# Filling the planned idle stretches of the matmul engine with unread identity products

## The chip, the cores and the metric

The kernel runs on one core of one Trainium2 chip. Times are device microseconds (us) from the first to the last instruction of that core and what lies around them; a shorter time is better. The core has a matmul engine (TensorE, PE in the profile; its weight loads are listed as PEld), a vector engine (VectorE, DVE), an activation engine (ScalarE, ACT), a general engine (GpSimd, POOL) and a queue that issues the DMAs (SyncE, SP). Each engine runs its own instructions in order and waits for others by semaphores. The profile also records the share of its full clock that PE is granted.

## The reference

The input x is 32 sequences of 256 tokens with 128 features, all fp32. Four blocks are applied, each behind a layer norm and each added to x:

```
x = x + attn_a(layernorm(x))   # delta-rule recurrence over the tokens, 128x128 state, gates
x = x + ffn(layernorm(x))      # silu(x Wg^T) * (x Wu^T), times Wd^T; integer weights / 127; hidden size 384
x = x + attn_b(layernorm(x))   # Mamba-2: in-projection, causal convolution of 4 taps, chunked state space, gated norm
x = x + ffn(layernorm(x))      # the same weights again
```

The recurrence of the first block, per sequence and token t, with k normalised and alpha, beta, g from sigmoids:

```
S = S @ (alpha_t * (I - beta_t * k_t k_t^T)) + beta_t * v_t k_t^T
o_t = (q_t @ S) * g_t
```

## The kernel before

**Tiling.** Two sequences (512 tokens, four tiles of 128) form a unit, and there are 16 units. A unit goes through attention (names ending in _a), the first feed-forward block (_f), the state-space block (_s) and the second feed-forward block (_h). Within the attention the recurrence is computed in blocks: a triangular system is inverted, first in blocks of 16 on DVE (tiles step_a and u_a, fed by rows_a through DRAM), then doubled on PE by transposes (pt_a) and pairs of products (p_a), with ACT copies between them (t_a). Layer norms end with a transpose of the normalised tile xn into xT_ps. Products are fp32 and each is two weight loads and two matmul instructions in the trace; transposes are one of each, with the identity matrix `ident` as the second operand.

**Memories.** Every PE result goes to one of eight PSUM banks (kind "ps", 512 fp32 per partition). A bank is taken by a tile at its first write and is free for the next tile when the last reader of the former is done.

**The order of the work.** No engine's order is written by hand. All operations of all units are first added as a graph (`add`), with an estimated busy time and latency for each. `matmul` estimates two passes of max(2n, 2 cols)/2.4 + 4.5 ns, which is 222 ns for a 128 x 128 product; `transpose` takes 109 ns. `Planner.run` (line 333) then simulates the engines: it repeatedly places the operation that can start first, by a key with units staggered (`SHIFT`, `STAGE`), and a start time that is the latest of the engine being free, the operands being ready, and a bank being free; for the first operation of a bank, also all operands that anything put into this bank will need (`b.gate`, line 385). The result is a start time `op.start` for each operation. The list is sorted by it (line 441), and the instructions are emitted in that order; each engine's program order is therefore the plan's. Times in the plan are used for the order alone: on the chip an instruction starts when its engine is there and its semaphores are.

Line 238 issues every product, line 251 every transpose, line 275 every DVE operation, lines 259 and 261 the ACT copies and activations, line 292 POOL's and line 302 the DMAs. Since these are helpers, one must go by the names of the tiles.

Of the kernel before, what the change touches and what calls it, by code (L numbers as in the profile page):

```python
# [18 lines left out]
P = 128  # L19
# [128 lines left out]
class Planner:  # L148
# [13 lines left out]
    RATE = 270.0  # L162
    LANES = 8
    CUT = 150.0
    KEEP = 3900.0
    SIZES = {"ps": 512, "m": 512, "l": 1024, "t": 64, "s": 32, "d": 512, "g": 8192, "b": 384, "e": 12288}

# [35 lines left out]
    def add(self, eng, busy, late, emit, outs, ins, table=None, after=(), lock=False):  # L203
        op = Op()
        op.eng, op.busy, op.late, op.emit, op.table, op.lock = eng, busy, late, emit, table, lock
        op.unit, op.n, op.stage = self.unit, len(self.ops), self.stage
        op.preds, op.succs, op.bufs = {p.n: p for p in after}, [], []
        op.moves, op.cut, op.batch = 0.0, 0, ()
        for v, write in [(v, False) for v in ins] + [(v, True) for v in outs]:
            if not isinstance(v, View):  # L210
                continue
            bits = v.bits()
            for other, obits, lanes, owrite in v.buf.seen:
                if (
                    other is not op and (write or owrite) and bits & obits
                    and lanes[0] < v.lanes[1] and v.lanes[0] < lanes[1]
                ):
                    op.preds[other.n] = other
            kept = v.buf.kind == "c" and not v.buf.again
            assert self.setup or not (kept and write)  # L220
            if self.setup or not kept:
                v.buf.seen.append((op, bits, v.lanes, write))
            if v.buf.kind == "c" and v.buf.tile is None:
                v.buf.tile = self.pools["c"].tile(list(v.buf.dims), v.buf.dtype, tag=v.buf.name, name=v.buf.name)
            if v.buf.kind != "c" and v.buf not in op.bufs:
                op.bufs.append(v.buf)
        for p in op.preds.values():
            p.succs.append(op)
        self.ops.append(op)
        return op  # L230
# [53 lines left out]
    def pool(self, name, out, *args, ins=(), cost=None, **kw):  # L284
        n = _count(out)
        if cost is None:
            cost = {
                "tensor_tensor": 1.66 * n + 149, "tensor_scalar": n + 260, "tensor_copy": n + 190, "memset": 0.97 * n + 60,
            }.get(name, n / 2 + 100)

        def emit():
            getattr(self.tc.nc.gpsimd, name)(real(out), *map(real, args), **{k: real(v) for k, v in kw.items()})  # L292

        lock = name == "tensor_tensor" and n > NT
        self.add("POOL", cost, 40, emit, [out], list(args) + list(kw.values()) + list(ins), lock=lock)
# [16 lines left out]
    def gates(self):  # L312
# [7 lines left out]
        for b, ops in users.items():  # L320
# [4 lines left out]
                    of.add(self.ops[n])  # L325
            b.gate = {p for op in ops for p in op.preds.values()} - of

    def at(self, unit):

        late = max(0, unit - (self.units - 3))  # L330
        return (unit - late + late * self.LAST) * self.period + self.SHIFT[unit]

    def run(self):
# [18 lines left out]
        free = dict.fromkeys(engines, 0.0)  # L352
# [9 lines left out]
        order = []  # L362
        while len(order) < len(ops):
            best = None
            for e in engines:
# [31 lines left out]
                if e == "PE":  # L397
                    same = [((k[0] + (self.KEEP if op.cut != cut else 0), k[1]), t, op) for k, t, op in same]
                pick = min(same, key=lambda x: x[0])
# [3 lines left out]
            t, op = best  # L403
# [4 lines left out]
            if op.eng == "PE":  # L408
                t += self.CUT if op.cut != cut else 0.0
                cut = op.cut  # L410
# [28 lines left out]
                oldest += 1  # L439
        self.span = max(op.done for op in ops)  # L440
        order.sort(key=lambda op: (op.start, op.n))
        with self.tc.manual_schedule():
            for op in order:
                for b in op.bufs:
                    if b.tile is None:
                        size = self.SIZES[b.kind]
                        flat = self.pools[b.kind].tile([1 if b.kind in "dge" else P, size], BF16 if b.kind in self.HALF else F32, tag=f"{b.kind}{b.slot[1]}", name=b.name + self.mark)
                        b.tile = flat[:, : b.size]
                        if len(b.dims) > 2:
                            names = " ".join(f"d{i}" for i in range(1, len(b.dims)))  # L450
                            b.tile = b.tile.rearrange(
                                f"p ({names}) -> p {names}", **{f"d{i}": b.dims[i] for i in range(2, len(b.dims))}
                            )
                op.emit()


# [5 lines left out]
def hybrid_block(ctx: ExitStack, tc: tile.TileContext, ins: dict, out: bass.AP):  # L462
# [36 lines left out]
    pl = Planner(tc, pools, period=17900.0, window=6)  # L499
# [6 lines left out]
            pattern=pattern, channel_multiplier=by,  # L506
        )

    ident = pl.const([P, P], "ident")
    pool("memset", ident, 0.0)  # L510
    select(ident, ALU.not_equal, 0, [[-1, P]], 1, fill=1.0)

# [186 lines left out]
    def power_half(dst, src, mul, add):  # L699

        n = dst.shape[1]
        pool("tensor_scalar", dst, src, mul, add, ALU.mult, ALU.add, cost=277)
        pool("tensor_tensor", dst, dst, neg_half[:, :n], ALU.pow, cost=350 + 160 * n)
# [33 lines left out]
    def attention(g, x):  # L737
# [117 lines left out]
        for b in range(NBLK):  # L855
            at = slice(b * BLOCK, (b + 1) * BLOCK)
            pl.dma(
                blocks[0, :].rearrange("(b t j i) -> b j t i", b=NBLK, t=NT, i=BLOCK)[b, :, :, :],
                diag[:, :, at].part(at), late=1400,
            )  # L860
        rows_n = pl.buf("l", [P, NT, BLOCK, BLOCK], f"rows_{n}")
        spread = rows_n.rearrange("p t j i -> p (t j i)")
        for b in range(NBLK):
            at = slice(b * BLOCK, (b + 1) * BLOCK)
            size = NT * BLOCK * BLOCK
            pl.dma(
                spread.part(at),
                blocks[0, b * size : (b + 1) * size].via(lambda ap: ap.partition_broadcast(BLOCK)),
                late=2100,
            )  # L870
# [374 lines left out]
```

## Time and profile before

| | |
|---|---|
| median of 3 runs | 804.33 us (802.57 to 809.08) |
| the profiled execution | 806.73 us |
| its span, first to last instruction | 804.9 us |
| mean granted clock of PE | 0.975 |
| instructions | 16786 |
| busy: PE, PEld | 744.7 us, 616.5 us |
| busy: DVE, ACT, POOL | 684.3, 597.2, 364.0 us |

Busy times are of one profiled execution. PE's records overlap one another, since a matmul starts before the last one has ended, and their ends are modelled; so a stretch in which PE reads as busy can still have room. A wait is listed as the instruction that waited, the engine and tile whose end released it, the total, the number of times and the longest. The chain is followed back from the last instruction to what released each step. A window's row gives start and end, length, and then for each engine the busy time and the instructions, the granted clock, the share of the DMA engines and GB/s.

### The profile page before, as it was taken

To read this page: it belongs to the slowest core of one execution; us is meant where nothing else is said; L and a number is where in the kernel's file an instruction comes from. 1 tells how busy PE (TensorE), PEld (TensorE's weight loads), DVE (VectorE), ACT (ScalarE), POOL (GpSimd) and SP (SyncE) were. 2 spreads that over 40 slices of the span, in tenths; PEclk is the share of its full clock that TensorE was granted. 3 is DMA by queue.
4 is the path that set the end of the run, shared out by engine and by line. 5 is a ranking of instruction groups with operands and counts; after the bars stand their busy time and mean duration, and the time that the engine had idled before them with its cause. 6 is when DMAs were issued, how large, how long until landed. Compare 5 with 4: busy or idle time off the path is not lost.

```text
span 804.9 us, 16786 instructions
## 1 busy us (share of the span) xinstructions
PE 744.7 (93%) x5485; PEld 616.5 (77%) x5485; DVE 684.3 (85%) x2386; ACT 597.2 (74%) x1443; POOL 364.0 (45%) x597
## 2 busy tenths in 40 slices
PE   5958999899999999999999999899999999998886
PEld 4646886687878888877988878686789988776775
DVE  4794799989988889889999689989898778999964
ACT  5833467979687877779787798897955578997862
POOL 8994332262452815514732634646631123243550
PEclk9976999999999999999999999999999999999999
DMA  5221110010110002101011002011201000000001
GB/s 145 82 68 42 29 42 1 5 33 1 56 30 24 22 7 67 42 27 33 18 30 31 27 15 58 16 45 44 67 4 43 14 5 1 5 15 5 13 10 44
DMA packets 42159, 25.48 MB, mean 32 GB/s; under 512 B 18448, under 2 KB 37840, under 8 KB 42064
## 3 DMA queue, kind: packets, MB, share of 16 engines
q1 hardware_dynamic: 41056, 24.13, 11.1%
q8 instruction: 45, 0.74, 0.4%
q14 instruction: 50, 0.41, 0.2%
q10 hardware_dynamic: 1008, 0.20, 0.1%
HBM read 19.16 MB, written 5.14 MB: 30 GB/s over the span
## 4 chain that ended last, share of the span: by engine, by line
PE 52%; DVE 20%; ACT 15%; POOL 5%; issue 3%; DMA 2%; SPq 1%; ACTq 0%; DVEq 0%; POOLq 0%
PE p_a L238 6%; PE fy_f L238 5%; DVE cy_s L275 4%; PE fy_h L238 4%; PE fg_f L238 3%; ACT L261 3%; PE sy_ps_s L238 3%; PE so_s L238 2%; PE fu_f L238 2%; PE pc_s L238 2%; PE fg_h L238 2%; PE fu_h L238 2%; PE pt_a L251 2%; DVE u_a L275 2%; PE cb_ps_s L238 2%
## 5 line engine op out<-in xcount | busy, mean ns | idle before, releaser
L275 DVE SCALAR_TENSOR_TENSOR cy_s<-pc_s,cw,cy_s 128x510 f32<-128x510 f32 (+2 forms) x192 | 137.6, 731 | 2.9 <-ACT cy_s L261 2.3
L261 ACT ACT_TABLE_LOAD x66 | 84.7, 1283 | 9.9 <-DMA x<-in_L_attn_a_x_dram 5.8
L238 PE MATMUL fy_f<-wdT,hT_f 128*128 128x128 f32 x384 | 74.5, 280 | 0.0
L238 PE MATMUL fy_h<-wdT,hT_h 128*128 128x128 f32 x384 | 72.1, 281 | 0.6 <-DVE hT_h L275 0.3
L238 PEld LDWEIGHTS fy_f<-wdT,hT_f 128*128 128x128 f32 x384 | 61.4, 191 | 6.3 <-issue 3.6
L238 PE MATMUL pc_s<-xT_s,w_xbc 128*128 128x512 f32 x128 | 64.5, 599 | 1.3 <-ACT gT_s L259 0.7
L238 PEld LDWEIGHTS fy_h<-wdT,hT_h 128*128 128x128 f32 x384 | 59.1, 191 | 8.1 <-issue 4.3
L275 DVE TENSOR_TENSOR step_a<-rows_a,u_a 128x16 f32<-128x16 f32 (+14 forms) x240 | 51.7, 216 | 7.5 <-DMA rows_a<-blocks_a 3.1
L275 DVE TENSOR_TENSOR u_a<-u_a,step_a 128x16 f32<-128x16 f32 (+14 forms) x240 | 54.3, 227 | 3.9
L261 ACT ACTIVATE cy_s<-pc_s,cb,cw 128x512 f32<-128x512 f32 x64 | 48.3, 779 | 9.3 <-PE pc_s L238 9.1
L292 POOL TENSOR_TENSOR xd_s<-xt_s,dt_s 128x512 f32<-128x512 f32 x32 | 33.2, 1045 | 42.9 <-ACT xt_s L259 42.2
L238 PE MATMUL so_s<-w_out,gT_s 128*128 128x128 f32 x256 | 45.8, 290 | 1.9 <-DVE cy_s L275 1.2
L238 PEld LDWEIGHTS so_s<-w_out,gT_s 128*128 128x128 f32 x256 | 39.7, 204 | 6.6 <-ACT cy_s L261 1.4
L261 ACT ACTIVATE sc_s<-cy_s 128x512 f32<-128x512 f32 x64 | 38.9, 636 | 3.6 <-DVE cy_s L275 1.9
L275 DVE SCALAR_TENSOR_TENSOR sm_s<-pl_s,cb_s 128x512 f32<-128x512 f32 x64 | 41.3, 680 | 0.3 <-ACT pl_s L261 0.2
L292 POOL TENSOR_TENSOR sy_s<-sy_s,yo_s 128x256 f32<-128x256 f32 x32 | 24.6, 773 | 35.5 <-DVE sy_s L275 14.2
L238 PEld LDWEIGHTS p_a<-t_a,neg_a 128*128 128x128 f32 x256 | 36.4, 203 | 5.5 <-ACT t_a L259 3.7
L238 PE MATMUL p_a<-t_a,neg_a 128*128 128x64 f32 x256 | 38.1, 280 | 1.8 <-DVE x L275 1.3
L238 PEld LDWEIGHTS p_a<-x_a,t_a 128*128 128x128 f32 x256 | 36.6, 201 | 3.7 <-ACT t_a L259 2.3
L238 PE MATMUL p_a<-x_a,t_a 128*128 128x64 f32 x256 | 37.9, 274 | 1.0 <-ACT t_a L259 1.0
L259 ACT COPY t_a<-pt_a 128x256 f32<-128x256 f32 (+1 forms) x64 | 20.2, 316 | 24.0 <-PE pt_a L251 22.9
L275 DVE TENSOR_TENSOR hT_f<-fth_f,fu_f 128x512 f32<-128x512 f32 x48 | 31.2, 681 | 7.3 <-PE fu_f L238 4.8
(253 smaller groups left out, 2420.7 us busy)
## 6 DMA issues: line engine op xcount, KB each, us to landing
rows_a<-blocks_a SPq DMA_DIRECT2D x128, 64.0 KB
x<-in_L_attn_a_x_dram SPq DMA_DIRECT2D x16, 256.0 KB
dec_a<-row_a SPq DMA_DIRECT2D x16, 256.0 KB
out_dram<-x SPq DMA_DIRECT2D x16, 256.0 KB
blocks_a<-neg_a SPq DMA_DIRECT2D x128, 4.0 KB
cuts_s<-cut_s SPq DMA_DIRECT2D x48, 8.0 KB
sums_t<-cuts_s SPq DMA_DIRECT2D x32, 12.0 KB
sums_s<-cuts_s SPq DMA_DIRECT2D x16, 24.0 KB
```

Source lines behind the costliest of these rows:

```text
L238: self.tc.nc.tensor.matmul(real(out), lhsT=real(lhsT), rhs=real(rhs), start=start, stop=stop)
L251: self.tc.nc.tensor.transpose(real(out), real(in_), real(ident))
L259: self.tc.nc.scalar.copy(real(out), real(in_))
L261: self.tc.nc.scalar.activation(real(out), real(in_), func, bias=real(bias), scale=real(scale), **kw)
L275: getattr(self.tc.nc.vector, name)(real(out), *map(real, args), **{k: real(v) for k, v in kw.items()})
L292: getattr(self.tc.nc.gpsimd, name)(real(out), *map(real, args), **{k: real(v) for k, v in kw.items()})
```

## The change

After the order is fixed, a new step walks through PE's operations in it. It keeps the time at which PE is free in the plan (starting at 1700 ns). Where the next operation's planned start is more than `IDLE` = 300 ns later, where its bank has not been written before by another PE operation, and where it isn't one of the half-width products (`op.cut`), the operation is marked with a number of extra products: int(gap x 0.7 / 223). When the program is emitted, these are issued just ahead of the operation: the identity (as stationary and as moving operand, at most 128 columns) into the start of the same bank. Nobody reads them; the operation then writes over them. The order of all other instructions is that of before, and no tile, bank, copy or DMA is added or moved.

```
+    IDLE, WARM = 300.0, 0.7
...
+    def keep_busy(self, order):
+        written, free = set(), 1700.0
+        for op in order:
+            if op.eng != "PE":
+                continue
+            bank = next(b for b in op.bufs if b.kind == "ps")
+            gap = op.start - free
+            if gap > self.IDLE and bank not in written and not op.cut:
+                op.warm, op.bank = int(gap * self.WARM / 223), bank
+            written.add(bank)
+            free = op.start + op.busy
...
         order.sort(key=lambda op: (op.start, op.n))
+        self.keep_busy(order)
...
-                        b.tile = flat[:, : b.size]
+                        b.flat = b.tile = flat[:, : b.size]
...
+                for _ in range(op.warm):
+                    n = min(P, op.bank.size)
+                    one = self.ident.real()
+                    self.tc.nc.tensor.matmul(op.bank.flat[:, :n], lhsT=one, rhs=one[:, :n], start=True, stop=True)
                 op.emit()
...
-    ident = pl.const([P, P], "ident")
+    ident = pl.ident = pl.const([P, P], "ident")
```

More of the change, by code (lines that the diff above doesn't have):

```diff
@@ L207, in add @@
         op.preds, op.succs, op.bufs = {p.n: p for p in after}, [], []
-        op.moves, op.cut, op.batch = 0.0, 0, ()
+        op.moves, op.cut, op.batch, op.warm = 0.0, 0, (), 0
         for v, write in [(v, False) for v in ins] + [(v, True) for v in outs]:
```

## The prediction

> **What bounds the kernel now.** I read the page first: engine totals, slices, the chain that ended last.
>
> ```profile
> PE 744.7 (93%) x5485; PEld 616.5 (77%) x5485; DVE 684.3 (85%) x2386; ACT 597.2 (74%) x1443; POOL 364.0 (45%) x597
> PEclk9976999999999999999999999999999999999999
> PE 52%; DVE 20%; ACT 15%; POOL 5%; issue 3%; DMA 2%; SPq 1%; ACTq 0%; DVEq 0%; POOLq 0%
> ```
>
> The matmul engine (PE) carries half of the chain and VectorE (DVE) a fifth. The granted clock is full almost everywhere; only the third and fourth of the 40 slices (about 40 to 80 us) fall to 0.7 and 0.6. Next I cut the span where the clock changes (columns: window, length, busy time and instruction count of PE, PE weight loads, DVE, ACT, POOL; then the clock, DMA share, GB/s):
>
> ```profile
> 48.00:58.20 10.20, 6.28 (x21) 5.02 (x22) 9.90 (x28) 2.82 (x6) 10.08 (x16) 0.50 0.21 67
> 65.00:78.60 13.60, 12.30 (x54) 11.27 (x55) 4.12 (x16) 3.65 (x11) 8.53 (x11) 0.50 0.22 61
> 242.50:246.00 3.50, 3.30 (x10) 2.62 (x11) 3.50 (x10) 3.48 (x8) 0.00 (x0) 0.52 0.00 0
> 730.60:734.00 3.40, 3.24 (x10) 2.36 (x11) 3.19 (x12) 2.42 (x8) 1.85 (x3) 0.50 0.00 0
> 754.50:758.00 3.50, 3.50 (x28) 3.28 (x29) 2.81 (x5) 3.44 (x5) 0.00 (x0) 0.52 0.00 0
> 771.50:775.00 3.50, 3.50 (x19) 3.36 (x17) 2.20 (x5) 1.87 (x2) 2.61 (x4) 0.51 0.02 5
> ```
>
> So PE runs at half clock in two long stretches near the start and four short ones. Each was preceded by a thin window; PE's records alone, busy in the 3.4 us ahead of a drop:
>
> ```profile
> 239.10:242.50 3.40, 2.15 (x10) 0.99 0.00 0
> 727.20:730.60 3.40, 1.39 (x13) 0.99 0.00 0
> 751.10:754.50 3.40, 1.84 (x10) 0.99 0.00 0
> 768.10:771.50 3.40, 1.59 (x24) 1.00 0.00 0
> 61.60:65.00 3.40, 1.53 (x7) 0.99 0.04 4
> ```
>
> Records 41 to 63% busy went before every drop. Last, the waits of PE over the whole run (total, times, longest), and the chain where the clock is half:
>
> ```profile
> PE kT_ps_a L251 <- POOL k_a L292: 4.5, 1, 4.5
> PE xT_ps_a L251 <- ACT xn_a L261: 3.3, 1, 3.3
> PE xT_ps_h L251 <- ACT cb_s L259: 2.2, 1, 2.2
> PE xT_ps_f L251 <- DVE cy_s L275: 1.9, 2, 1.2
> PE fu_f L238 <- ACT fth_f L261: 1.3, 1, 1.3
> ```
> ```profile
> 64.96 1.98 PE p_a L238 x8
> 67.39 1.99 PE p_a L238 x8
> 69.95 1.11 PE pt_a L251 x4
> ```
>
> The first two wait for their own operands. The other three wait for something the matmul doesn't read (an xT transpose reads neither cb nor cy, fu_f doesn't read fth_f): the last reader of the PSUM bank that the new tile takes over. That difference decides what a filler is worth.
>
> **What the Trainium skill says.** (1) "TensorE: Matmul & The Clock Gate", section "What's actually happening": the array's clock is halved after an idle window of about 3.4 us, and restored after a busy one. The trace agrees: the short dips last 3.4 to 3.5 us, the long ones are 10.2 (three windows) and 13.6 (four). (2) Same page, "Part 4: PE-mode transpose": transposes don't count as PE activity in the same way. The trace fits without proving it: from 65.0 to 78.6 records are busy 12.30 of 13.6 us, transposes (pt_a, kT_ps_a) among them, and the clock stays at half for four windows. (3) "Perfetto Trace Analysis", section "Identifying the Most-Contended Engine": matmul busy time is a poor measure of headroom, weight-load busy time a better one; here they are 93% and 77%, so PE has free places that the first hides. (4) "PSUM — Partial Sum Buffer", section "Terms": two engines on one bank's quadrant at once is an error, so a filler has to wait for the bank's readers as the real product does. The bank waits above agree.
>
> **The change, part by part.** The order, the buffers, every other instruction and every DMA queue stay: keep_busy only reads the finished plan, and nothing is moved.
>
> *What is added.* Ahead of an operation that is the first to write its bank, where the plan leaves over 300 ns, int(0.7 x gap / 223 ns) products of the identity with itself. Each fp32 product is two weight loads and two matmuls.
>
> *Price of one.* Eight p_a matmuls (four products) follow one another at 84.86 to 85.80 in 0.94 us with the clock full, so 0.23 us; at half clock eight start at 71.58 and the next product at 73.34, so 0.44 us. I use 0.223 warm (the plan's figure, which this supports) and 0.44 cold.
>
> *How many.* The plan's gaps are in no view; I take PE's idle in the trace as the nearest, and put both ends. Between 80 and 720 us PE has 24 us of idle (615.97 busy of 640) in some 45 gaps; a record also holds about 0.16 us of latency (a p_a matmul lasts 0.27 to 0.28 us and starts 0.11 after the last) that the plan counts as gap: 24 + 45 x 0.16 = 31 us. All filled: 0.7 x 31 / 0.223 = 98 products. Rounding down, gaps ahead of an operation that isn't first in its bank, and a plan that is tighter than the run cut it; ends 30 and 120, I take 50. Up to 80 us: 5.8 us ahead of the first product (plan start counted from 1.7) make 18, the waits of 4.5 and 3.3 make 14 and 10, the small ones some 12. After 720 us: six waits, 7 us, up to 22.
>
> *Cost in the middle.* 50 x 0.223 = 11 us of PE work. A filler ahead of an operand wait lies in idle time, if plan and run agree; one ahead of a bank wait can start only when the bank is free, and then delays the real product by its whole length, with all later PE work queued behind it, and ACT or DVE waiting for its result. I take half as late, 5.5 us, and let PE's share of the chain (52%) pass it on: **+3**. Ends: 30 products, a third late: +1; 120, three quarters late, 70% passed on: +14.
>
> *Gain at 65 to 79.* This is on the chain: p_a at half clock, 54 matmul records in 13.6 us, of which half would be saved if PE were the only thing there; less the ACT and DVE pieces, about 6 us. Whether the clock holds at 65.0 depends on the window 61.6 to 65.0. Fillers ahead of pvq_a (0.9 us of wait), pd_a (0.4) and p_a (0.55), some six products, 1.3 us, would bring its 1.53 us of records to 2.9 of 3.4, above every window that dropped. I take **-4**: six by two chances in three. Ends 0 and -6. What is late next is the DVE step and update chain and the SP issues at 93, which follow from these products and so move with them.
>
> *Gain at 48 to 58:* nothing. The waits there become filled, but DVE is busy 9.90 of 10.2 us and carries the chain (step_a, u_a, e_a); if that cover were gone, the cold kk_a group (2.77 us against 1.47 a little later) would be worth 1.3 us.
>
> *Before the first product:* PE idles until 8.05 us and then works cold until 17.2. The 18 fillers take 18 x 0.44 = 8 us cold, less once warm: the first real product is 0.3 us late at most by my sum, but pv_a and pk_a on the chain (12.86 to 16.5) may run at full clock, worth 1.8 us. From 19.5 to 37 the chain is POOL without a break, and hides most of it: **-1**, ends -2 and +1.
>
> *The end, 720 to 802.* Fillers ahead of xT_ps_h and pl_s (bank waits, 2.2 and 1.2 us) come after the release: 7 + 4 products, 2.5 us, with half on the chain, 1.3 us. Against that, three dips at half clock cost up to 1.7 us each; so_s at 754.5 and 772.7 is on the chain. Fillers ahead of pf_s (operand wait, 1.8 us) can prevent the last one. Together **-1**, ends -4 and +3.
>
> *Sum:* +3 - 4 - 1 - 1 = -3 us. The profiled execution took 806.73 us (span 804.9 plus 1.8 around it), so 803.7; the median of the runs is 804.33, 2.4 below the profiled one. I give it on the median: **801**.
>
> **Rivals.**
> A (the forecast, 0.41): the clock gain at the start outweighs a modest PE load: 801.
> B, slower (0.29): bank waits. Most plan gaps are bank waits, or don't fall where the run idles, so the fillers queue in front of real work. 100 products, 22 us, three quarters late, 70% passed on: +12, less 3 of clock gains: 813. For it: of PE's five longest waits three are for a bank's reader, and PE is half of the chain. Against: 24 us of idle exist in the middle. It decides from about 60 late products on (60 x 0.223 x 0.52 = 7 us against 6 of gain).
> C, faster (0.24): all fills land in idle time and all six stretches run at full clock: -1.5 at the start, -6 at 65 to 79, -3.5 later, +1: 794. For it: each drop follows a thin window; against: bank waits at the last dips.
> D (0.06): the change does little: the plan has few gaps above 300 ns, or the clock drops all the same, as the transposes may not count: 804.
>
> **How the numbers follow.** About 1% is what a measurement of this kernel can tell from no change (the three runs span 802.6 to 809.1). The range takes in most of B and C: 792 to 815; it leaves out the worst end of the middle's cost (+14 with no gain, 818) and C with its last dips all gone. Faster by over 1% (below 796.3): most of C and the gain's upper end in A, 0.29. Slower by over 1% (above 812.4): half of B and a bit, 0.23. Within: 0.48.
>
> **What would show it.** The page's PE row: 5485 plus twice the products, 5700 to 5900. Clock: 1.00 in 65 to 79 and 48 to 58 if A or C is right; then the p_a groups take about 1.0 us and not 1.97, and everything after 80 us starts some 4 us sooner. For B: identity products that start right after a bank's release, with a real product directly behind, and a lead at 80 us that melts by 720. The forecast is wrong if the clock at 65 still drops, if that lead is swallowed by DVE or POOL (idle ahead of rows_a would grow), or if the plan holds over 100 products in the middle.

## The result: slower by 0.6%, and the profile after

Twenty-two runs of each kernel give a median of 809.28 us after (806.14 to 813.02) and 804.76 us before. The ratio is **1.0058**, with a 95% interval of 1.0040 to 1.0076: slower by 3.2 to 6.1 us. (Here and below a ratio is estimated from the single runs of both kernels; it can differ from the quotient of the two medians by about 0.1%.) The profiled execution of the changed kernel took 809.79 us (span 808.0), against 806.73 us (span 804.9) before: 3.1 us more. Its mean granted clock rose all the same, from 0.975 to 0.990.

The page after: busy time and instructions, PE's clock in 40 slices, and the shares of the chain that ended last.

```profile
PE 761.3 (94%) x5713; PEld 635.4 (79%) x5713; DVE 684.8 (85%) x2386; ACT 597.2 (74%) x1443; POOL 364.4 (45%) x597
PEclk9997999999999999999999999999999999999999
PE 48%; DVE 22%; ACT 16%; POOL 6%; issue 3%; DMA 3%; SPq 2%; DVEq 0%; ACTq 0%; POOLq 0%
```

PE has 228 instructions more, so 114 extra products. DVE, ACT and POOL do the same work as before. The third slice is now at full clock, the fourth still shows 0.7. The windows of the kernel after that still run at half clock, apart from the first 7.2 us (the clock's record starts there; that PE is slow ahead of it shows in the weight loads of the extra products, 333 ns instead of 192) and the last 2 us, in which PE does nothing (columns as in the prediction: window, length, busy time and instructions of PE, PE weight loads, DVE, ACT, POOL, then the clock):

```profile
61.80:72.10 10.30, 10.10 (x41) 8.24 (x41) 4.61 (x18) 4.06 (x16) 8.80 (x15) 0.50 0.31 74
734.30:737.70 3.40, 3.40 (x17) 3.34 (x17) 1.36 (x4) 0.00 (x0) 1.08 (x2) 0.50 0.00 0
```

The stretch at 48 to 58 is gone, the one that the prediction wanted gone (65 to 79 before) has moved to 61.8 and lasts three windows instead of four, and one of the four short dips is left in this execution. PE's waits after (total, times, longest):

```profile
PE pvq_a L239 <- DVE neg_a L276: 3.3, 1, 3.3
PE xT_ps_h L473 <- ACT cb_s L260: 2.2, 1, 2.2
PE xT_ps_f L473 <- DVE cy_s L276: 1.7, 2, 1.1
PE fu_f L473 <- ACT fth_f L262: 1.2, 1, 1.2
```

Line 473 is that of the extra products. **They wait for the same releases as the real operations did**: xT_ps_h still waits 2.2 us for cb_s, fu_f 1.2 us for fth_f, about as long as before (2.2 and 1.3). Such a wait isn't filled; the products merely come behind it. And a new long wait has appeared, pvq_a for neg_a. It was 0.9 us before, and has no extra product ahead of it.

**Where the time went.** I followed the start of the same instructions in both traces. The changed kernel is 1.1 us ahead at 40 to 50 us, 3.5 at 59, again 1.1 at 63, when the wait for neg_a is over, and 2.8 us ahead at 80 (the product wq_a starts at 78.49 instead of 81.27). The lead is 0.7 us at 140 to 160, 0.4 at 200 to 230 and 1.4 at 250 to 290; then it is behind by 1.2 at 340, 1.5 at 480, 2.7 at 520, 3.0 at 640 to 700, 5.9 at 740 and 3.0 again at 780. So 2.8 us are won by 80 us and 5.8 us lost from there to 700. Of these 5.8 us, 2.6 fall in 296 to 340 us, where no extra product stands; they come back under the hardware below. At extra products the lead shrinks, or the lag grows, by 1.6 us from 133 to 148 us (12 of them, ahead of pz_s, xT_ps_f, pt_a, fg_f and fu_f), by 0.3 at 188 (2 ahead of so_s), 0.6 at 520 to 523 (5 ahead of so_s and p_a) and 0.1 at 554 (1 ahead of cs_s): together 2.6 us. What else is lost, some 1.6 us in four small steps, has no extra product or a single one at its place, and 0.9 us is won where the dip of before at 242 us is missing.

In the plan, 58 products stand in the first 70 us and 56 later. Of the 56, **39 stand ahead of an operation whose planned start is within 50 ns of the time at which its PSUM bank comes free**, and 17 ahead of other operations. By the trace, 35 of the 56 run between 80 and 720 us, 23 of them of the bank kind.

### The profile page after: what moved, and what is told of

It reads as the page before. It is cut to its first block, busy times and chain, and to the rows that moved or that the text cites. A ratio compares the mean times of both kernels' runs of the same rounds, so it can differ in the third digit from the quotient of the medians.

```text
span 808.0 us, 17232 instructions
## 1 busy us (share of the span) xinstructions
PE 761.3 (94%) x5713; PEld 635.4 (79%) x5713; DVE 684.8 (85%) x2386; ACT 597.2 (74%) x1443; POOL 364.4 (45%) x597
## 4 chain that ended last, share of the span: by engine, by line
PE 48%; DVE 22%; ACT 16%; POOL 6%; issue 3%; DMA 3%; SPq 2%; DVEq 0%; ACTq 0%; POOLq 0%
PE p_a L239 6%; DVE cy_s L276 4%; PE fy_f L239 4%; PE fy_h L239 3%; PE pc_s L239 3%; ACT L262 3%; PE fg_f L239 2%; PE fu_h L239 2%; PE fu_f L239 2%; PE fg_h L239 2%; PE sy_ps_s L239 2%; PE so_s L239 2%; SPq L303 2%; DVE u_a L276 2%; PE pt_a L252 2%
## 5 line engine op out<-in xcount | busy, mean ns | idle before, releaser
L276 DVE TENSOR_TENSOR step_a<-rows_a,u_a 128x16 f32<-128x16 f32 (+14 forms) x240 | 53.4, 223 | 10.4 <-DMA rows_a<-blocks_a 5.3
L239 PE MATMUL so_s<-w_out,gT_s 128*128 128x128 f32 x256 | 42.9, 276 | 0.0
L239 PEld LDWEIGHTS so_s<-w_out,gT_s 128*128 128x128 f32 x256 | 37.3, 192 | 3.3 <-issue 1.2
L262 ACT ACTIVATE pl_s<-pl_s 128x512 f32<-128x512 f32 x64 | 33.8, 581 | 5.3 <-PE pl_s L239 5.2
```

The lines of the kernel that those rows point to most:

```text
L239: self.tc.nc.tensor.matmul(real(out), lhsT=real(lhsT), rhs=real(rhs), start=start, stop=stop)
L262: self.tc.nc.scalar.activation(real(out), real(in_), func, bias=real(bias), scale=real(scale), **kw)
L276: getattr(self.tc.nc.vector, name)(real(out), *map(real, args), **{k: real(v) for k, v in kw.items()})
```

## The experiments

Two theories. **T1 (bank):** a stretch in which PE is idle because no bank is free can't be filled through that same bank. The products start at the release, and the real product starts later by their whole length. **T2 (load):** any extra product costs some PE time, as plan and run don't agree on where the gaps are; a cheap wait and a dear one don't differ. Beside these, for the early part: **T3**, the gain was to be had, but the planned gaps didn't put products in front of the window that decided it.

The kernels below differ from the changed kernel only in which operations get products. For this, `run` records when the plan found the bank free. All compute the whole reference, and ratios are to the kernel before, on the same chip.

### The early products alone

```
+                    if b.kind == "ps":
+                        op.slot_at = b.slot[0]
...
+            for_bank = op.start - op.slot_at < 50.0
-            if gap > self.IDLE and bank not in written and not op.cut:
+            if gap > self.IDLE and bank not in written and not op.cut and op.start < 70000.0:
```

> Only the 58 products of the first 70 us of the plan stay. Theory (what costs is a product that waits for the bank of the product behind it, later on): PE is full-clocked from about 7 us, p_a is reached some 2.8 us sooner as in the changed kernel's profile, and nothing takes it away later: 2 to 3 us under the kernel before, ratio 0.9965. Rival (extra PE work costs wherever it stands, about half of 0.223 us each): 58 products, 13 us, hidden in the start or not, +2 us or more. Second rival (a start that is sooner is swallowed by DVE or POOL): within 0.1% of before.

Measured: 802.89 us, ratio 0.9980 (0.9952 to 1.0009), so -1.6 us, and no change isn't excluded. In this execution the clock was at half from 62.1 to 86.0 us, and wq_a started at 82.07, later than in the kernel before:

```profile
62.10:86.00 23.90, 23.51 (x101) 21.36 (x100) 9.08 (x36) 7.25 (x27) 9.72 (x15) 0.50 0.15 35
```

The early products don't hold the clock at 62 us. The lead of 2.8 us that the changed kernel showed at 80 us is the property of one execution.

### Only the products ahead of bank waits, and only the others

```
-            if gap > self.IDLE and bank not in written and not op.cut:
+            if gap > self.IDLE and bank not in written and not op.cut and for_bank:
```

> Only products ahead of an operation that the plan holds back for a free bank (start within 50 ns of the time at which the bank comes free): 39 products, all after 115 us of the plan. Theory: each starts when the bank is free and delays the real product by its whole 0.223 us: 8.7 us of delay, of which nearly all reaches the end, less some 3 us of clock dips near the end that they prevent: +5 to +6 us, ratio 1.006 to 1.0075. Rival (extra PE work costs about the same wherever it stands): 39 of 114 products, a third of the measured +4.6 us, so +1.5 us.

```
+            if gap > self.IDLE and bank not in written and not op.cut and not for_bank:
```

> The other 75 products: those of the first 70 us and 17 later ones whose operation the plan holds back for operands or for the bank's other operands. Theory: 2 to 4 us under the kernel before, ratio 0.995 to 0.9975, as fast as the early ones alone or a little faster. Rival (cost by number): 75 of 114, +3 us, ratio 1.004.

Measured: the 39 bank products alone give 810.53 us, **1.0083** (1.0059 to 1.0107), +6.7 us, a little over what was expected. The 75 others give 805.19 us, 1.0009 (0.9988 to 1.0030), +0.7 us. The loss is therefore in the 39, as T1 wants. The second run missed its expectation of 0.995 to 0.9975: the 17 late products that aren't ahead of bank waits eat the 1.6 us of the early ones, or the intervals hide it; this pair doesn't tell. The two kernels share out all 114 products of the change, and 6.7 + 0.7 = 7.4 us is 2.7 more than the 4.7 of the change. The intervals (1.9, 1.7 and 1.4 us to either side) just cover that gap, so a part can't be read more finely than to 2 or 3 us from medians.

### The bank products doubled

```
-                op.warm, op.bank = int(gap * self.WARM / 223), bank
+                op.warm, op.bank = int(gap * 2 * self.WARM / 223), bank
```

(with `for_bank` as above: 87 products)

> As the run with only the products ahead of bank waits, but with twice the share of the gap: 87 products in place of 39. Theory: the cost grows with PE time behind the release: 87 x 0.223 = 19.4 us, less the same 3 us of dips: +14 to +16 us, ratio 1.018 to 1.020. Rival (the cost is one of a wait moved onto another instruction, or of the program's length, not of PE time): about as the single share, +5 us.

Measured: 815.67 us, 1.0130 (1.0095 to 1.0165), +10.5 us. A miss: 48 further products are 48 x 0.223 = 10.7 us of PE time and cost only 3.8 us. One place explains a part of it. These are PE's instructions ahead of xT_ps_h in this run and in the changed kernel (start, duration, engine, line, tile, count, and the idle before with its releaser):

```profile
740.78 2.94 PE L477 MATMUL xT_ps_h<-ident 128*128 128x128 f32 x24 [2.18 <-ACT cb_s L260]
743.56 0.60 PE L252 MATMUL xT_ps_h<-ident,xn_h 128*128 128x128 f32 x4
```
```profile
734.09 2.81 PE L473 MATMUL xT_ps_h<-ident 128*128 128x128 f32 x12 [2.20 <-ACT cb_s L260]
736.70 1.06 PE L252 MATMUL xT_ps_h<-ident,xn_h 128*128 128x128 f32 x4
```

Twelve products (24 instructions) at full clock delay the transposes by 743.56 - 740.78 = 2.78 us, six at half clock by 736.70 - 734.09 = 2.61. By the medians the further products weigh less than the first ones: 39 pass on 6.7 of 8.7 us, 87 pass on 10.5 of 19.4 us. The traces don't bear this out at the places of the products. Up to 720 us the lag behind the kernel before grows there by 2.6 of 5.1 us with the 23 products of the undoubled rule, and by 7.5 of 11.8 us with the 53 of the doubled one. What the doubled kernel's trace lacks is loss at other places: nothing from 285 to 345 us, where that of the undoubled kernel loses 2.0 us without a product. Six runs and one trace don't settle whether the miss comes from that.

### The bank products of the middle alone, and as many ahead of operand waits

```
+            if gap > self.IDLE and bank not in written and not op.cut and for_bank and op.start < 660000.0:
```

> Of the 39 products ahead of bank waits, only the 23 of the middle (plan 115 to 660 us); the 16 of the last part are left out. Theory: 23 x 0.223 = 5.1 us of delay behind a release, about two thirds of it passed on: +3 to +4 us, ratio 1.004 to 1.005. Rival (the cost of the 39 is that of the last part, where six products ahead of xT_ps_h run at half clock): +1 us or less, ratio under 1.0015.

The counterpart has no planned products. A list of tile names gives 23 of them, all between 80 and 720 us, to operations that wait for their own operands in the trace:

```
+    HOLD = {"p1_a0_64": 1, "py_a0": 1, "p3_a2_64": 1, "py_a2": 3, "pt_a5_16": 4, "py_a4": 1, "xT_ps_f4": 4, ...}
...
+            if bank not in written and bank.name in self.HOLD:
+                op.warm, op.bank = self.HOLD[bank.name], bank
```

> 23 products in the middle, as many as in the run with the bank waits of the middle alone (ratio 1.0063), but ahead of other operations: 13 of which PE waits in the trace of before for an operand that they read, with their bank free (p1_a0_64 1, py_a0 1, p3_a2_64 1, py_a2 3, pt_a5_16 4, py_a4 1, xT_ps_f4 4, p3_a5_64 1, pz_s7_0 1, z_a9 1, p3_a11_16 1, p3_a11_64 1, pf_s11_0 3). Theory: they lie in the idle time and cost next to nothing: ratio 0.999 to 1.0015. Rival (PE is the bound in the middle, and any product there costs about the same): 1.005 to 1.007.

Measured: ahead of bank waits 810.42 us, **1.0063** (1.0041 to 1.0084), +5.1 us, over the +3 to +4 that was expected; ahead of operand waits 805.80 us, **1.0017** (0.9994 to 1.0040), +1.4 us. The PE time added is the same, 23 x 0.223 = 5.1 us. By the middle values the bank products cost as much as all of it, the operand products a quarter, and for these nothing isn't excluded. The intervals just don't overlap: equal PE time doesn't cost the same, so T2 falls and T1 stands. The traces show why. First two waits of the kernel before, then the same places in the kernel with bank products (PE's timeline, line 477 the products, idle in brackets):

```profile
142.52 0.63 PE L251 MATMUL xT_ps_f<-ident,xn_f 128*128 128x128 f32 x4 [1.16 <-DVE cy_s L275]
148.57 0.50 PE L238 MATMUL fu_f<-xT_f,wuT 128*128 128x512 f32 x1 [1.30 <-ACT fth_f L261]
```

```profile
142.12 1.16 PE L477 MATMUL xT_ps_f<-ident 128*128 128x128 f32 x8 [1.06 <-DVE cy_s L276]
143.11 0.60 PE L252 MATMUL xT_ps_f<-ident,xn_f 128*128 128x128 f32 x4
...
149.14 0.94 PE L477 MATMUL fu_f<-ident 128*128 128x128 f32 x6 [1.18 <-ACT fth_f L262]
149.83 0.48 PE L239 MATMUL fu_f<-xT_f,wuT 128*128 128x512 f32 x1
```

PE is idle for 1.06 us, until cy_s, the last reader of the bank's former tile, has ended. Then come the products, and directly behind them, with no idle, the transposes that could have started at 142.12. Next the kernel with operand products (line 480):

```profile
237.74 1.06 PE L480 MATMUL xT_ps_f<-ident 128*128 128x128 f32 x8
238.98 1.10 PE L253 MATMUL xT_ps_f<-ident,xn_f 128*128 128x128 f32 x3 [0.18 <-ACT xn_f L263]
...
579.25 0.83 PE L480 MATMUL pf_s<-ident 128*128 128x128 f32 x6
580.16 0.70 PE L240 MATMUL pf_s<-xe_s,cb_s 128*128 128x256 f32 x2
```

Here the brackets have changed sides. The products have no idle before them and start as soon as PE is done with the last operation; the transposes behind still wait 0.18 us for xn_f. The wait for xn_f was 1.1 us before. They took idle time and delayed nothing. At one of the 13 places it was otherwise: the three products ahead of py_a at 132 us waited 0.71 us themselves, for oT_a, and py_a came directly behind.

**How much of the cost lies at the products.** The lag behind the kernel before, followed by the start of the same instructions, grows in the trace with bank products by 1.6 us from 135 to 151 us (12 products), 0.3 at 190 (2), nothing at 375 (3), 0.6 at 522 to 526 (5) and 0.1 at 556 (1): 2.6 of the 5.1 us. A delay of PE can thus vanish before it reaches the end, as at 375. In the trace with operand products it grows by less than 0.05 us at each of the 13 places, that of py_a included. Both traces lose more where no product stands, near 300, 340, 421, 500 and 622 us: 5.2 and 4.3 us. So most of the difference between the two kernels is at the products (2.6 us by the traces, of 3.7 by the runs); of the +5.1 us, about half isn't shown to be theirs.

A rival is that one kernel simply ran longer at half clock than the other. The granted clock of each run is on record. An estimate takes the time at half clock out by a straight line through the runs of both kernels and of the kernel before (0.37 and 0.39 us for each us; one run is left out, see below): +4.9 us (4.1 to 5.7) and +2.5 us (1.9 to 3.2) remain. The difference stays.

### Products where the clock fell

The changed kernel's trace ahead of its half-clock stretch (PE's timeline):

```profile
57.64 0.60 PE L252 MATMUL pt_a<-ident,x_a 128*128 128x128 f32 x4
61.54 0.91 PE L239 MATMUL pvq_a<-xT_a,gT_a 128*128 128x256 f32 x2 [3.30 <-DVE neg_a L276]
63.88 1.97 PE L239 MATMUL p_a<-t_a,neg_a 128*128 128x64 f32 x8
```

Between 58.2 and 61.5 us PE has nothing, as pvq_a waits for a bank that neg_a still reads; at 61.8 the clock falls, and the p_a group takes 1.97 us as before. A product in pvq_a's own bank would come too late. So the products were put one operation further up, into the bank of pt_a, which is free: 12 there, 1 ahead of pd_a, 2 ahead of the first p_a.

```
+    HOLD = {"pt_a1_16": 12, "pd_a5": 1, "p1_a1_16": 2}
```

(with the early products, `op.start < 70000.0`)

> The early 58 products, and 15 more that the plan does not ask for: 12 ahead of the transpose pt_a that runs at 57.6 us in the changed kernel's profile (after it PE waits 3.3 us for a bank), 1 ahead of pd_a and 2 ahead of the first p_a group. Theory (the half clock at 62 to 65 us follows from that idle stretch, and how long it lasts is a matter of where the clock's window happens to lie): the clock is 1.00 from about 7 us to at least 80, all p_a groups take 1.0 to 1.1 us, p_a is some 4 to 5 us sooner than in the kernel before: ratio 0.993 to 0.996, and the runs scatter less. Rival (the clock drops all the same, since transposes or waits in 60 to 80 us bring it down): half clock between 62 and 80 as before, ratio 0.998 like the early products alone.

And the same without the 26 products ahead of the first operations:

```
+            if gap > self.IDLE and bank not in written and not op.cut and 20000.0 < op.start < 70000.0:
```

> As the run that holds the clock, without the 26 products before 11 us. Theory (POOL hides what happens before 37 us, so that the early clock there is worth 1 us at most): ratio within 0.002 of the run that holds the clock, 0.994 to 0.997. Rival (the gain of the early products is that of the first full-clock stretch, 7 to 17 us): the gain is gone, ratio 0.998 to 1.000.

Measured: 801.28 us, **0.9943** (0.9923 to 0.9963), -4.6 us; and without the first ones 799.78 us, **0.9931** (0.9906 to 0.9956), -5.6 us. The latter's trace at the same place, and its windows from 51.1 to 80 us:

```profile
59.02 2.84 PE L480 MATMUL pt_a<-ident 128*128 128x128 f32 x24
61.70 0.60 PE L253 MATMUL pt_a<-ident,x_a 128*128 128x128 f32 x4
62.48 0.67 PE L240 MATMUL pvq_a<-xT_a,gT_a 128*128 128x256 f32 x2 [0.18 <-DVE neg_a L277]
64.11 0.61 PE L480 MATMUL p_a<-ident 128*128 128x128 f32 x4
64.82 1.10 PE L240 MATMUL p_a<-t_a,neg_a 128*128 128x64 f32 x8
```
```profile
51.10:80.00 28.90, 27.52 (x194) 23.34 (x193) 23.11 (x74) 10.21 (x33) 17.36 (x28) 1.00 0.15 43
```

The 12 products stand ahead of pt_a, and pvq_a behind it still waits 0.18 us for its bank, so that they lie in what was idle time. The clock stays full, the p_a group takes 1.10 us instead of 1.97, and wq_a starts at 76.45 instead of 81.27. T3 stands: the early part was forecast at -5 us (-4 for 65 to 79, -1 ahead of the first product). It gives -4.6 with both, and -5.6 without the products ahead of the first operations, when products are at this place; the change didn't put them there. The interval of the early products alone (0.9952 to 1.0009) overlaps these two a little, but the granted clock of the single runs agrees: 0.986 to 0.996 in all 34 runs of the two kernels, 0.974 to 0.989 in the 14 of the early products alone. The second run came out below its expected 0.994 to 0.997.

### The same for the end

```
+    HOLD = {"pt_a1_16": 12, "pd_a5": 1, "p1_a1_16": 2, "gT_ps_s14_0": 3, "pf_s15_0": 7}
```

> As the run that holds the clock without the products before 11 us (ratio 0.9931), and 10 products more in operand waits near the end: 3 ahead of gT_ps_s14_0 (0.8 us of wait before) and 7 ahead of pf_s15_0 (1.8 us). Theory: they cost nothing and prevent the last short drop of the clock where it would come (1.7 us at most): ratio 0.991 to 0.993, the fastest of all. Rival (the drop near the end comes from the bank waits ahead of it too, or hides behind ACT and POOL): 0.993 to 0.994, no different.

Measured: 799.93 us, 0.9935 (0.9910 to 0.9959), no different from the run without it, as the rival had it. After 80 us the clock still fell three times in the profiled execution, at 237.9, 726.0 and 749.9 us; the last:

```profile
749.90:753.30 3.40, 3.40 (x31) 3.18 (x31) 2.64 (x5) 3.34 (x5) 0.00 (x0) 0.50 0.00 0
```

There was no dip later in this execution; whether one was kept away by the products or fell elsewhere by chance can't be told from it.

### Summary

| products | number | ratio | us on 804.8 |
|---|---|---|---|
| the change | 114 | 1.0058 (1.0040 to 1.0076) | +4.7 |
| early alone | 58 | 0.9980 (0.9952 to 1.0009) | -1.6 |
| ahead of bank waits | 39 | 1.0083 (1.0059 to 1.0107) | +6.7 |
| all but these | 75 | 1.0009 (0.9988 to 1.0030) | +0.7 |
| ahead of bank waits, doubled | 87 | 1.0130 (1.0095 to 1.0165) | +10.5 |
| ahead of bank waits, before 660 us | 23 | 1.0063 (1.0041 to 1.0084) | +5.1 |
| ahead of operand waits, 80 to 720 us | 23 | 1.0017 (0.9994 to 1.0040) | +1.4 |
| early, and ahead of pt_a, pd_a, p_a | 73 | 0.9943 (0.9923 to 0.9963) | -4.6 |
| the same without the first 26 | 47 | 0.9931 (0.9906 to 0.9956) | -5.6 |
| the same, and two places at the end | 57 | 0.9935 (0.9910 to 0.9959) | -5.2 |

The 39 and the 58 add up to 6.7 - 1.6 = +5.1 us, against +4.7 for the change; this leaves 17 products out, and with them (the 39 and the 75) it is +7.4. The three versions with products at pt_a beat both kernels; which of the three is best can't be told.

## Why the prediction was wrong

The forecast was 801 us, and 809.28 was measured: rival B's side of the range, near its 813: 7.7 us above the forecast of -3. By the runs above, three terms make up about this much: 3.4 us where the early part gave -1.6 instead of -5, 2.1 us in the middle, and 2.6 us at the end, which is the least certain. By the steps of the forecast:

- **Count of instructions: right.** 5713, in 5700 to 5900.
- **The middle, +3: too small, by a loss that the sum had no term for.** It took 50 products, half of them late, so 5.5 us of delay, and passed on 52%. There were 35 between 80 and 720 us, 23 of them ahead of bank waits: fewer products and a larger late share, which by luck make nearly the same delay, 5.1 us. These 23 alone cost +5.1 us (3.3 to 6.8). At their own places the trace keeps 2.6 us of it, so about the half that the forecast passed on; place by place, though, it is anything from nothing (at 375 us) to more than half (at 135 to 151), and PE's share of the chain isn't shown to be the reason. What the sum put at nothing is loss away from the products: "nothing is moved", and yet 5.2 us were lost in that trace where none stands, and 4.3 with the operand products. What causes this stays open. The mechanism, a filler behind a bank's release that delays what comes behind it, was read rightly, but from a list with a gap: the five waits shown aren't PE's five longest. wT_ps for rstd_a (8.1 us) and pf_s for xe_s (2.6) belong among these, so one of the five longest was for a bank's reader, not three.
- **65 to 79 us, -4: this step failed, in the placement.** It put "some six products" ahead of pvq_a, pd_a and p_a, into the window that decides. The plan had none ahead of pvq_a, pd_a or the first p_a group; the next one, a single product, stands behind that group, when the clock has already fallen. The gaps are those of the plan's own clock, and the wait of 0.9 us in the trace wasn't one of them; it was also a wait for a bank, so a product in that bank would have come behind it. In the profiled execution, with the half-clock stretch at 48 to 58 gone and PE ahead, the wait ahead of pvq_a grew from 0.9 to 3.3 us, a thinner window than before. The whole early part measured -1.6 us (-3.9 to +0.7), and -4.6 and -5.6 once 15 products stood at the right place. The mechanism and its size were right; the change lacked the products for it. (The statement that records 41 to 63% busy went before every drop leaves out the drop at 48.0 us, with 17%.) "The plan's gaps are in no view; I take PE's idle in the trace as the nearest" is the assumption that fell.
- **48 to 58 us, nothing: agrees with what was seen.** The clock was full there in the changed kernel, and the lead, 1.1 us at 40 to 50 us, was 1.1 us again at 63.
- **Before the first product, -1: nothing was gained.** The plan put 22 products there, not 18, and the first real product started 1.26 us later (9.31 us instead of 8.05), not 0.3. The clock was full from 7.2 us instead of 17.2, and yet, with products at pt_a in both, the kernel without these early ones is no slower (799.78 against 801.28 us).
- **The end, -1: not seen, and by the runs rather a loss.** The 39 bank products cost 6.7 us and the 23 of them in the middle 5.1, which leaves +1.6 us for the 16 at the end, with an error of over 2 us. In the profile it is about nothing. The lag is 3.0 us at 700 and 3.1 at the end. Between them the six products ahead of xT_ps_h ran at half clock and cost 2.6 us; the lag went from 5.9 us back to 3.0 where two dips of before, at 754 and 771, weren't there. As the late dips fall at other places in each trace, that can't be put down to the change.
- **Rival B** had the right mechanism and place, and the sign that it named was seen: products right after a release, the real product directly behind, and a lead at 80 us that was gone by 720 (2.8 us ahead, 3.0 behind at 700). Its number came near by a different sum: it had 100 products at a cost of 12 us and 3 us of gain; there were 35 in the middle, and 1.6 us of gain. Its turning point of "about 60 late products" was too high: it reckoned with 0.52 x 0.223 us for each, and 39 in fact cost 6.7 us, 0.17 each by the median; and the gain of 6 us that they were to outweigh wasn't there.

## What to carry to other kernels

Ask of every idle stretch what it waits for: if the instruction reads what released it, work can be put in front of it; if it only takes over a buffer from the instruction that released it, work in that buffer comes behind the wait and delays it. Fillers for the clock belong in front of the one window that decides a half-clock stretch on the chain, in a buffer that is free at that time, and that place is found in the trace, not in a plan. Fifteen products there, added to the early ones, turned a gain of 1.6 us that can't be told from nothing into one of 4.6. The 56 later ones of the change turned the same 1.6 us into a loss of 4.7.

## What the runs showed of the hardware that I had not expected

**The clock comes back late, and not always after the same time.** From 20 us to the last product, all half-clock stretches here have lengths of about 3.4 us times a whole number, but how many follow one drop varies between programs that are identical up to that time. With no product before 80 us, the stretch near 65 us lasted 13.6 us (before), 6.8 (bank products), 23.9 (doubled), 13.6 (bank products of the middle) and 13.6 (operand products). The shortest and the longest (windows of the bank products and of the doubled ones):

```profile
69.00:75.80 6.80, 6.55 (x30) 6.16 (x31) 2.61 (x7) 1.36 (x5) 4.20 (x5) 0.50 0.44 116
```
```profile
63.40:87.30 23.90, 22.36 (x93) 19.94 (x94) 9.09 (x37) 7.03 (x25) 9.29 (x12) 0.50 0.14 35
```

PE is busy for 22.36 of 23.9 us by its records, and the clock isn't restored for seven windows. "TensorE: Matmul & The Clock Gate", section "What's actually happening", has the clock at full again after at least one busy window of about 3.4 us, and at half after at least one idle window. By PE's records this trace differs on the first, and the measurement decides: seven windows weren't enough. On the second, a window ahead of a drop need not be idle: in the kernel with 73 products one with 2.61 of 3.40 us in records (from 235.1 us) was followed by half clock. Transposes and products of 64 columns are among the records; whether these are counted less wasn't tried. The start of wq_a follows: 81.27, 78.53, 82.60, 80.73 and 80.54 us. A gain of 3 us at 80 us in one profile is within this scatter. One and the same program scatters too: in 110 runs of the kernel before that were made beside the experiments the mean granted clock went from 0.966 to 0.983, and most of the spread of its times goes with it (19 runs at 0.982 have a median of 802.6 us, 7 at 0.974 one of 807.3). A straight line gives 0.36 us for each us at half clock, with a correlation of 0.84. One run of the bank products of the middle, left out above, lies far off such a line: 0.936 and 810.15 us. With the products at the right place (three kernels) the stretch was absent each time and wq_a started at 75.75 to 76.45.

**DMA issues stall, and the loss can sit at the same place in several programs.** In 296 to 340 us the changed kernel lost 2.6 us with no extra product there. SP's timeline before and after, the same eight DMAs:

```profile
296.31 3.69 SPq L302 DMA_DIRECT2D blocks_a<-neg_a  x8
```
```profile
294.95 4.95 SPq L303 DMA_DIRECT2D blocks_a<-neg_a  x8
```

One issue of some 0.42 us took 1.3 us longer; a group of eight at 329 us (rows_a) did so too, 4.81 instead of 3.66 us. Of SP's 436 issues, five last over 0.8 us in the trace before and nine in the trace after, mostly at different DMAs (in each trace one is at 89 us). The stretch from 285 to 345 us costs 2.0 to 2.6 us in the changed kernel's trace and in five others: bank products, those of the middle, all but the bank products, operand products, and the kernel with 73. The last three have no bank product. In the other four traces, the doubled bank products among them, it costs nothing. So the bank products aren't the cause; what decides it isn't shown. A loss of a microsecond or two between two single traces isn't evidence by itself, and a loss that comes with one program and not with another can pass for a cost of the change. The comparison of 22 runs each, and the pair of 23 against 23, carry the conclusion here.
